# The first layer of an image network on one time scale instead of rounds, with one image kept on chip

## The chip, the cores and the metric

The kernel runs on one core of a Trainium2 chip. It computes two layers of an image network in float32 in one launch. The metric is the device time of one execution in microseconds, as the median of a few runs. Engines are named as in the profile: PE (matrix engine; PEld its weight loads), DVE (vector engine), ACT (scalar engine), POOL, and SP, which issues most DMAs. All engines run their own queue of instructions in order[...].

## What is computed

The input `x` has 4 images of 192 channels and 128 x 128 points. Both layers have the form `x + f(gn(x))`, where `gn` normalises groups of six channels over all points of an image:

```python
x = x + _L0_conv_ref(_gn(x), ...)   # first layer: transforms of the image plane
x = x + _L1_conv_ref(_gn(x), ...)   # second layer: a scan over the 16384 points of an image
return x
```

The first layer is what the change touches:

```python
x1 = c1x1(x, conv1_w)                                   # 192 -> 48 channels
x_0, x_05, x_1 = x1[:, :16], x1[:, 16:32], x1[:, 32:48]
Fre = frft2d(x_05, 0.5)                                 # fractional Fourier transform of the plane
mag, pha = abs(Fre), angle(Fre)
mag_out = c1x1(c3x3(mag * mask1, ...) * mask1 + c1x1(mag * mask2, ...) * mask2, ...)
pha_out = c1x1(pha, ...)
ifrft = abs(frft2d(complex(mag_out * cos(pha_out), mag_out * sin(pha_out)), -0.5))
# x_1: rfft2, a 1x1 convolution of magnitude and of phase, irfft2;  x_0: a 1x1 convolution
return c1x1(concatenate([x_0o, ifrft, x_1o], axis=1), conv2_w)      # 48 -> 192 channels
```

The second layer is a state-space scan (384 inner channels, 16 states) over the points in order, with a normalisation over channels, two projections and a gate around it.

## The kernel before

`layer0` treats an image in four works, each a Python generator that emits some instructions and yields:

- **analysis** (line 266): sixteen pieces of `x` (96 partitions, 2 x 1024 points, 768 KB each) are loaded by SP (`load`, line 196) and their statistics taken on DVE (`bn`, line 202). After all sixteen, `bn_done` (line 215) makes the group statistics, which are folded into the weights of the 1x1 convolution (L284 to L291). Then every piece is convolved (L301) on PE, evacuated by ACT (L305) into one of two `x1` buffers, and stored in the DRAM tensor `d1` from ACT's queue (L311). The last four pieces (`KEEP = 4`) are still on chip from the first pass. The other twelve are loaded again.
- **forward** (line 314): one read of `d1` (`img<-d`, L317), then the transforms on PE (L233, L243) with copies on ACT (L249) and DVE (L251), and `_polar` (L70 to L100: magnitude and phase, much of it on DVE, with a reciprocal at L87). Magnitudes and phases are stored in DRAM (L326, L333).
- **backward** (line 337): the 3x3 and 1x1 convolutions (L263, L373), `_from_polar` (L103 to L119, with five operations of a block on DVE ahead of ACT's sines and two behind), a store and a read with rows and columns exchanged (L397, L425, L417, L453), then the inverse transforms (L432, L440, and L462, L470 for the second kind), and the store `dimg<-img` (L478).
- **synthesis** (line 481): for each of sixteen pieces it reads `d1` and `dimg` into one of two `cat` tiles (L492, L493), projects 48 to 192 channels (L506), adds the result to a piece of `x` loaded once more (L510), takes the statistics that the second layer needs (L205), and stores the sum (`xmid<-xt`, L514, from POOL's queue). At its end `bn_done` makes this image's statistics `st2`.

The pieces of `x` of analysis and synthesis share one pool of seven buffers, `l0x`. The tiles of transforms lie in the pools `l0i`, `l0z`, `l0u`, `l0v` and `l0q`, all opened before any work begins.

The order of emission is set by rounds. `weave` (line 520) takes several works with a number of steps each, spreads the steps evenly, and at the end of the round runs every work to its end. Image 0's analysis comes first and alone. Then round `p` holds backward of image `p - 1`, forward of image `p`, analysis of image `p + 1` and synthesis of image `p - 2`:

```python
for p in range(B + 1):
    works = []
    if p:
        works.append((backward(p - 1, got[p - 1]), 19))
    if p < B:
        works.append((forward(p, got[p]), 9))
    if p + 1 < B:
        works.append((analysis(p + 1, got[p + 1]), 2 * NPIECE + 1))
    if p >= 2:
        works.append((synthesis(p - 2, got[p - 2], []), NPIECE + 1))
    weave(works, early if p == B else None)
```

In the last round the first four pieces of the last synthesis are loaded early, at step 14 of 19 (`LOADS`). A scheduler below takes the order of emission as priority, and from it makes the fixed queue of each engine, which may differ in detail. The last synthesis runs after the rounds, beside the preamble of the second layer (`layer1`: constants, `group_norm`, the first chunk of 512 points). From there on `layer1` follows a plan written out by hand (`PLAN`), under manual scheduling; its loop of scans (`tensor_tensor_scan`, L989) takes the rest of the time.

Of the kernel before, what the change touches and what calls it, by code (L numbers as in the profile page):

```python
# [33 lines left out]
NPIECE = S // ROWS  # L34
# [87 lines left out]
def layer0(tc, x, xmid, st2, w):  # L122

    nc = tc.nc
    B = x.shape[0]
    KEEP = 4
    LOADS = 14
    with ExitStack() as ctx, ExitStack() as inner:
        def pool(name, bufs, ctx=inner, **kw):
            return ctx.enter_context(tc.tile_pool(name=name, bufs=bufs, **kw))  # L130

        kp = pool("l0k", 1, ctx)
        dram = pool("l0d", B, ctx, space=DRAM)
        xp = pool("l0x", 7, ctx)
        sp = pool("l0s", 2, ctx)
        psB = pool("l0r", 2, ctx, space=PSUM)
        cp = pool("l0c", 1)
        fp = pool("l0f", 2)
        imp = pool("l0i", 2)
        zp = pool("l0z", 2)  # L140
        up = pool("l0u", 7)
        vp = pool("l0v", 4)
        qp = pool("l0q", 1)
        psA = pool("l0p", 4, space=PSUM)

        def const(name, cp=cp):
# [46 lines left out]
        def split(v):  # L193
            return v.rearrange("(t p) f -> p t f", p=CH)

        def load(b, p):
            xt = xp.tile([CH, 2, PIECE], F32, name="xt")
            src = x[b].rearrange("c h w -> c (h w)")[:, p * PIECE : (p + 1) * PIECE]
            nc.sync.dma_start(out=xt, in_=split(src))
            return xt  # L200
# [56 lines left out]
        def by_row(d, c0, nch):  # L257
            return d[c0 * S : (c0 + nch) * S, :].rearrange("(c k) l -> k c l", k=S)
# [4 lines left out]
            nc.tensor.matmul(ps[:, 0:n], bd[:, i, :], rhs, start=True, stop=True)  # L263
            return ps[:, 0:n]

        def analysis(b, got):


            st = sp.tile([CH, 2, NPIECE * (PIECE // 512), 6], F32, name="st")
            kept = {}  # L270
            for p in range(NPIECE):
                xt = load(b, p)
                if p >= NPIECE - KEEP:
                    kept[p] = xt
                bn(st, p, xt)
                yield
            gst = sp.tile([CH, 2, 2], F32, name="gst")
            bn_done(st, gst, in_a)

            w1r = fp.tile([CH, 2, 128], F32, name="w1r")
            for t in range(2):
                nc.vector.tensor_scalar(w1r[:, t, :], w1T[:, t, :], gst[:, t, 1:2], None, ALU.mult)  # L284
            ps = psA.tile([128, 512], F32, name="ps")
            for t in range(2):
                nc.tensor.matmul(
                    ps[:, 0:1], w1r[:, t, :], gst[:, t, 0:1], start=t == 0, stop=t == 1
                )
            b1 = fp.tile([128, 1], F32, name="b1")  # L290
            nc.vector.tensor_scalar(b1, ps[:, 0:1], -1.0, None, ALU.mult)  # L291
            d1 = got["d1"] = dram.tile([3 * NC, S * S], F32, name="d1")
            for p in (*range(NPIECE - KEEP, NPIECE), *range(NPIECE - KEEP)):
                xt = kept.pop(p, None) or load(b, p)
                if p % 2 == 0:
                    x1 = fp.tile([128, 2, 512], F32, name="x1")
                ps = psA.tile([128, 512], F32, name="ps")
                for t in range(2):
                    for q in range(2):
                        half = slice(64 * q, 64 * (q + 1))  # L300
                        nc.tensor.matmul(  # L301
                            ps[half], w1r[:, t, half], xt[:, t, q * 512 : (q + 1) * 512],
                            start=t == 0, stop=t == 1,
                        )
                nc.scalar.activation(x1[:, p % 2, :], ps, AF.Identity, bias=b1)  # L305
                if p % 2 == 1:
                    at = d1[:, (p - 1) * PIECE : (p + 1) * PIECE].rearrange(
                        "c (e q f) -> q c e f", e=2, q=2
                    )
                    for q in range(2):  # L310
                        nc.scalar.dma_start(out=at[q], in_=x1[64 * q : 64 * q + 3 * NC])  # L311
                yield

        def forward(b, got):

            xT = imp.tile([128, 2 * NC, S], F32, name="img")
            nc.sync.dma_start(out=xT, in_=got["d1"][NC:, :].rearrange("c (h w) -> h c w", h=S))  # L317

            dm = dmag[b % len(dmag)]
            dp = got["dp"] = dram.tile([NC * S, S], F32, name="dp")  # L320
            for half in range(2):
                mag, pha = yield from spectrum(
                    xT, 0, fr2[:, 0, :], fr2, S, (2 * half, 2 * half + 1)
                )
                for src, dst in ((mag, dm[1 : NC * S + 1, :]), (pha, dp)):
                    nc.sync.dma_start(  # L326
                        out=by_row(dst, 8 * half, 8), in_=src.rearrange("k (c l) -> k c l", c=8)
                    )

            dh = got["dh"] = [dram.tile([NC * S, L], F32, name=f"dh{i}") for i in range(2)]  # L330
            polar = yield from spectrum(xT, NC, rf1, rf2, L, range(4))
            for src, dst in zip(polar, dh):
                nc.sync.dma_start(  # L333
                    out=by_row(dst, 0, NC), in_=src.rearrange("k (c l) -> k c l", c=NC)
                )
# [145 lines left out]
        def synthesis(b, got, early):  # L481

            d1, dimg = got["d1"], got["dimg"].rearrange("c h w -> c (h w)")
            st = sp.tile([CH, 2, NPIECE * (PIECE // 512), 6], F32, name="st2")
            xts = list(early)

            def fetch(p):
                if p < NPIECE:
                    cat = cats[p % 2]
                    for q in range(2):  # L490
                        at = slice(p * PIECE + q * 512, p * PIECE + (q + 1) * 512)
                        nc.sync.dma_start(out=cat[64 * q : 64 * q + NC, :], in_=d1[0:NC, at])  # L492
                        nc.sync.dma_start(out=cat[64 * q + NC : 64 * q + 3 * NC, :], in_=dimg[:, at])  # L493
                if len(early) <= p + len(early) < NPIECE:
                    xts.append(load(b, p + len(early)))

            if early:
                fetch(0)
            for p in range(NPIECE):
                fetch(p + 1 if early else p)  # L500
                xt, cat = xts[p], cats[p % 2]
                for t in range(2):
                    pr = psB.tile([128, 2, 512], F32, name="pr")
                    for q in range(2):
                        rows = slice(64 * q, 64 * q + 3 * NC + 1)
                        nc.tensor.matmul(  # L506
                            pr[0:CH, q, :], w2x[rows, t * CH : (t + 1) * CH], cat[rows, :],
                            start=True, stop=True,
                        )
                    nc.vector.tensor_add(  # L510
                        xt[:, t, :], xt[:, t, :], pr[0:CH].rearrange("p q f -> p (q f)")
                    )
                bn(st, p, xt)
                nc.gpsimd.dma_start(  # L514
                    out=split(xmid[b][:, p * PIECE : (p + 1) * PIECE]), in_=xt
                )
                yield
            bn_done(st, st2[:, b], in_b)

        def weave(works, early=None):  # L520

            n = max(count for _, count in works)
            for i in range(n):
                for work, count in works:
                    for _ in range((i + 1) * count // n - i * count // n):
                        next(work, None)
                if early is not None and i == LOADS:
                    early.extend(load(B - 1, p) for p in range(KEEP))
            for work, _ in works:
                for _ in work:  # L530
                    pass

        got = [{} for _ in range(B)]
        weave([(analysis(0, got[0]), 1)])
        early = []
        for p in range(B + 1):
            works = []
            if p:  # L540
                works.append((backward(p - 1, got[p - 1]), 19))
            if p < B:
                works.append((forward(p, got[p]), 9))
            if p + 1 < B:
                works.append((analysis(p + 1, got[p + 1]), 2 * NPIECE + 1))
            if p >= 2:
                works.append((synthesis(p - 2, got[p - 2], []), NPIECE + 1))
            weave(works, early if p == B else None)
        inner.close()
        yield  # L550
        yield from synthesis(B - 1, got[B - 1], early)
# [730 lines left out]
```

## Time and profile before

| what | value |
|---|---|
| runs of the kernel before | 10828.12, 10829.38, 10840.17 us; median 10829.38 |
| the profiled execution, its own time | 10830.13 us |
| its span, first to last instruction | 10828.4 us |
| mean granted PE clock | 0.957 |
| busy over the span | PE 91%, DVE 94%, ACT 87%, POOL 85% |
| first 1400 us | 293 MB moved by DMA (209 GB/s) of 1417 MB in all |
| in these, most of it | `xt<-in_x` 176 loads of 768 KB; `xmid<-xt` 64 stores of 768 KB |

A row of the table of stages gives the stretch in us, its length, then for each engine the busy time in us with the number of instructions in brackets, and last the granted PE clock (1.00 is full speed), the mean busy share of the 16 DMA engines and the rate in GB/s. A row of a timeline gives start and duration in us, engine, source line, operation, output and inputs with shapes, and the number of instructions merged in it. In square brackets stands how long the engine was idle before it and what ended that. `SPq` is SP's queue issuing DMAs, so its duration is that of issuing, not of the transfer. One matrix product in float32 shows as two MATMUL records, so a piece's convolution (four products) shows as x8.

### The profile page before, as it was taken

Reading aid. Unit: us, or ns where it says so; the run is one execution under the profiler, and the core shown is the slowest. Engines: PE = TensorE matmul, PEld = TensorE weight load, DVE = VectorE, ACT = ScalarE, POOL = GpSimd, SP = SyncE. Lnnn points to the kernel's source line nnn. Section 1 sums busy time; section 2 is a strip of 40 time slices with the busy share of each in tenths; the row PEclk is TensorE's granted clock in tenths of the full one; section 3 lists DMA queues with packets and bytes.
Section 4 is the critical chain, followed back from the end, with each engine's and each line's share of the span. In section 5 each row is a group of like instructions: output and inputs, shape, how many; then the busy total and the mean of one; then the engine's idle time right before and its main releaser. Section 6 shows DMA issues by size and latency. Waiting matters only on the chain.

```text
span 10828.4 us, 170277 instructions
## 1 busy us (share of the span) xinstructions
PE 9879.0 (91%) x55538; PEld 6942.9 (64%) x55538; DVE 10219.2 (94%) x11587; ACT 9404.2 (87%) x19559; POOL 9214.5 (85%) x4214
## 2 busy tenths in 40 slices
PE   4776789999999999999999999999999999999998
PEld 2444366666666666666666666666666666666666
DVE  4666699999999999999999999999999999999999
ACT  1332189999999999999999999999999999999998
POOL 0000089999999999999999999999999999999999
PEclk8888799999999999999999999999999999999999
DMA  8786743443443443443444444444444344344343
GB/s 229 189 227 179 222 137 108 126 127 108 127 124 111 124 125 112 122 126 112 120 127 113 118 127 116 115 127 118 113 127 122 109 127 123 109 127 126 108 127 98
DMA packets 1357320, 1416.75 MB, mean 131 GB/s; under 512 B 920729, under 2 KB 972174, under 8 KB 1355790
## 3 DMA queue, kind: packets, MB, share of 16 engines
q1 hardware_dynamic: 1335950, 1342.94, 44.5%
q0 software_dynamic: 13312, 50.34, 1.4%
q10 hardware_dynamic: 7168, 12.59, 0.4%
q8 instruction: 440, 7.21, 0.3%
q14 instruction: 450, 3.69, 0.1%
HBM read 1230.12 MB, written 155.33 MB: 128 GB/s over the span
## 4 chain that ended last, share of the span: by engine, by line
PE 50%; ACT 19%; DVE 17%; issue 5%; DMA 1%; POOL 0%; SPq 0%; DVEq 0%; POOLq 0%; ACTq 0%
PE ps L799 18%; PE ps L1015 14%; DVE h L989 11%; ACT da L911 6%; PE op L975 5%; DVE op L932 3%; PE ps L1055 3%; ACT dbT L960 3%; ACT L696 2%; ACT op L911 1%; ACT L818 1%; PE ps L1030 1%; ACT zs L818 1%; ACT sT L758 1%; DVE st L732 1%
## 5 line engine op out<-in xcount | busy, mean ns | idle before, releaser
L1002 POOL TENSOR_TENSOR hc<-h,c 128x1024 f32<-128x1024 f32 x3072 | 7202.9, 2367 | 314.5 <-DVE h L989 249.2
L989 DVE TENSOR_TENSOR_SCAN h<-da,carry,op 128x512 f32<-128x512 f32 x4712 | 5821.6, 1265 | 8.6 <-issue 2.9
L911 ACT ACTIVATE da<-dt,c_A_log 128x512 f32<-128x512 f32 x4864 | 3423.7, 751 | 219.5 <-DVE h L989 199.1
L1015 PE MATMUL ps<-ident,hc 128*128 128x128 f32 x24576 | 3221.3, 277 | 4.1 <-POOL hc L1002 4.1
L1015 PEld LDWEIGHTS ps<-ident,hc 128*128 128x128 f32 x24576 | 2866.7, 144 | 411.8 <-issue 402.0
L960 ACT ACTIVATE dbT<-ps,bT 128x128 f32<-128x128 f32 x8192 | 2291.2, 399 | 32.7 <-PE op L975 23.3
L799 PE MATMUL ps<-s,wc 128*128 128x512 f32 x4608 | 2142.3, 596 | 18.8 <-ACT s L784 13.9
L932 DVE TENSOR_TENSOR op<-ps,b 128x512 f32<-128x512 f32 x2816 | 1897.0, 674 | 5.7 <-ACT ps L892 5.7
L975 PE MATMUL op<-ident,dbT 128*128 128x128 f32 x8192 | 1319.6, 292 | 445.3 <-DVE h L989 417.9
L989 DVE TENSOR_TENSOR_SCAN h<-op,carry,db 128x512 f32<-128x512 f32 x1240 | 1547.3, 1267 | 6.9 <-ACT op L911 1.3
L943 POOL TENSOR_TENSOR db<-dtu,b 128x1024 f32<-128x1024 f32 x640 | 1514.1, 2366 | 6.2 <-DMA xmid<-xt 6.2
L975 PEld LDWEIGHTS op<-ident,dbT 128*128 128x128 f32 x8192 | 1034.0, 151 | 745.2 <-DVE h L989 437.3
L799 PEld LDWEIGHTS ps<-s,wc 128*128 128x128 f32 x4608 | 804.0, 190 | 725.0 <-issue 681.2
L911 ACT ACTIVATE op<-dt,c_A_log 128x512 f32<-128x512 f32 x1280 | 928.9, 726 | 14.1 <-DVE h L989 14.1
L1055 PE MATMUL ps<-yg,c_woT 128*96 128x512 f32 x1536 | 700.9, 592 | 0.0
L696 ACT ACT_TABLE_LOAD x511 | 655.6, 1283 | 9.8 <-PEq L1272 0.7
L514 POOL DMA_DIRECT2D xmid<-xt x64 | 41.7, 651 | 576.0 <-DVE xt L510 491.5
L857 POOL TENSOR_TENSOR dtu<-dt,u 128x512 f32<-128x512 f32 x384 | 482.5, 1271 | 0.0
L205 DVE BATCH_NORM_STATS2 st<-xt 96x6 f32<-96x512 f32 x512 | 322.6, 677 | 106.7 <-DMA xt<-in_x 105.5
L78 POOL TENSOR_TENSOR u<-u 128x1024 f32<-128x1024 f32 (+1 forms) x12 | 29.7, 2475 | 453.0 <-ACT u L77 453.0
L1055 PEld LDWEIGHTS ps<-yg,c_woT 128*96 128x96 f32 x1536 | 236.6, 163 | 273.1 <-issue 273.1
L1030 PE MATMUL ps<-ddp,u 128*128 128x128 f32 x3072 | 405.8, 275 | 0.0
(175 smaller groups left out, 10012.2 us busy)
## 6 DMA issues: line engine op xcount, KB each, us to landing
c<-dbc SPq DMA_DIRECT2D x1024, 512.0 KB, 4.9
b<-dbc SPq DMA_DIRECT2D x768, 512.0 KB, 6.1
xt<-in_x SPq DMA_DIRECT2D x176, 768.0 KB, 8.6
xmid<-xt POOLq DMA_DIRECT2D x64, 768.0 KB, 6.2
xm<-xmid SPq DMA_DIRECT2D x128, 384.0 KB, 3.9
carry<-h SPq DMA_DIRECT2D x3072, 1.0 KB, 2.0
xr<-xmid SPq DMA_DIRECT2D x128, 384.0 KB, 3.8
out<-xr SPq DMA_DIRECT2D x128, 384.0 KB, 3.9
```

The lines of the kernel that those rows point to most:

```text
L696: nc.scalar.preload_act_table_set("natural_log_exp_and_others")
L799: nc.tensor.matmul(g["c", j][0], wc[:, j, k, :], rhs, start=k == 0, stop=k == 5)
L911: nc.scalar.activation(da, got[n]["dt", j], AF.Exp, scale=A[:, j, st : st + 1])
L932: nc.vector.tensor_tensor(dbs[s], g["dp", j][0], g["b", k % NG][:, q, :], ALU.mult)
L943: nc.gpsimd.tensor_tensor(db, _bc(g["dtu", j], 1, G), g["b", sg], ALU.mult)
L960: nc.scalar.activation(t[:, blk, :], g["tu", j][0][:, at], AF.Identity, scale=g["bT"][:, blk, st : st + 1],)
L975: nc.tensor.transpose(db[:, blk * 128 : (blk + 1) * 128], t[:, blk, :], ident)
L989: nc.vector.tensor_tensor_scan(h[:, q, :], das.pop(s), dbs.pop(s) if db is None else db[:, q, :], 0.0 if ch == 0 else g["before"][:, j, st ...
L1002: nc.gpsimd.tensor_tensor(hc, h, g["c", sg], ALU.mult)
L1015: nc.tensor.matmul(py[:, blk, :], hc[:, q, blk * 128 : (blk + 1) * 128], ident, start=first, stop=sg == NG - 1 and q == G - 1 and blk == N ...
L1030: nc.tensor.matmul(got[n]["py", j][0][:, blk * 128 : (blk + 1) * 128], got[n]["u", j][:, blk * 128 : (blk + 1) * 128], ddp[:, j, :], start ...
L1055: nc.tensor.matmul(po, woT[:, j, t * CH : (t + 1) * CH], g["yg", j], start=j == 0, stop=False)
```

## The change

Four things change, all in `layer0`:

- Image 0 is kept on chip. For its analysis alone, a second pool `l0y` of nine buffers is opened, so all sixteen pieces have a place (nine there, seven in `l0x`) and no piece is loaded twice. The pools of the transforms are opened only after that, in the same space. The six last pieces are convolved first, then the other ten.
- `weave` and the rounds are gone. Every work has a begin and an end on one time scale, where image `b`'s forward lies from `b + 0.05` to `b + 0.95`, its backward from `b + 1` to `b + 2`, its synthesis from `b + 2` to `b + 2.9`, and its analysis from `b - 1.1` to `b - 0.15` (image 0's runs ahead of all). A work's steps are spread evenly between, and all steps are sorted by time. A round's end no longer runs the works to their ends.
- So analysis begins a tenth of a round sooner and ends 0.15 sooner, forward begins later by 0.05 and ends sooner by as much, and synthesis ends a tenth sooner.
- The early loads of the last synthesis come at 4.74 on that scale.

```diff
-    LOADS = 14
+    ANALYSIS, FORWARD, BACKWARD, SYNTHESIS = (-.1, .85), (.05, .95), (1, 2), (2, 2.9)
+    LAST_LOADS = 0.74
+    XBUFS = 7
...
-        def analysis(b, got):
+        def analysis(b, got, more=None):
...
+            keep = NPIECE if more else KEEP
             for p in range(NPIECE):
-                xt = load(b, p)
-                if p >= NPIECE - KEEP:
+                xt = load(b, p, more if more and p < NPIECE - XBUFS else xp)
+                if p >= NPIECE - keep:
                     kept[p] = xt
...
-            for p in (*range(NPIECE - KEEP, NPIECE), *range(NPIECE - KEEP)):
+            last = NPIECE - (XBUFS // 2 * 2 if more else KEEP)
+            for p in (*range(last, NPIECE), *range(last)):
                 xt = kept.pop(p, None) or load(b, p)
...
+        got = [{} for _ in range(B)]
+        with tc.tile_pool(name="l0y", bufs=NPIECE - XBUFS) as more:
+            for _ in analysis(0, got[0], more):
+                pass
+        imp = pool("l0i", 2)
...
+        works = [(B + LAST_LOADS, B + LAST_LOADS, 1, loads)]
+        for b in range(B):
+            if b:
+                works.append((*(b - 1 + t for t in ANALYSIS), 2 * NPIECE + 1, lambda b=b: analysis(b, got[b])))
+            works.append((*(b + t for t in FORWARD), 9, lambda b=b: forward(b, got[b])))
+            works.append((*(b + t for t in BACKWARD), 19, lambda b=b: backward(b, got[b])))
+            if b < B - 1:
+                works.append((*(b + t for t in SYNTHESIS), NPIECE + 1, lambda b=b: synthesis(b, got[b], [])))
+        steps = sorted(
+            (begin + (i + 1) * (end - begin) / count, n, i)
+            for n, (begin, end, count, _) in enumerate(works) for i in range(count)
+        )
+        running = [make() for *_, make in works]
+        for _, n, i in steps:
+            next(running[n], None)
+            if i + 1 == works[n][2]:
+                for _ in running[n]:
+                    pass
```

More of the change, by code (lines that the diff above doesn't have):

```diff
@@ L133, in layer0 @@
         dram = pool("l0d", B, ctx, space=DRAM)
-        xp = pool("l0x", 7, ctx)
+        xp = pool("l0x", XBUFS, ctx)
         sp = pool("l0s", 2, ctx)
@@ L138, in layer0 @@
         fp = pool("l0f", 2)
[L139 to L143, printed above, removed]
         psA = pool("l0p", 4, space=PSUM)
@@ L194, in split, with load @@
             return v.rearrange("(t p) f -> p t f", p=CH)
-        def load(b, p):
+        def load(b, p, xp=xp):
             xt = xp.tile([CH, 2, PIECE], F32, name="xt")
@@ L518, in synthesis @@
             bn_done(st, st2[:, b], in_b)
[L520 to L530, printed above, removed]
-                    pass
@@ L535, in layer0 @@
[L535 to L548, printed above, removed]
+        got = [{} for _ in range(B)]
@@ new lines, in layer0, with loads @@
+        with tc.tile_pool(name="l0y", bufs=NPIECE - XBUFS) as more:
+            for _ in analysis(0, got[0], more):
+                pass
+        imp = pool("l0i", 2)
+        zp = pool("l0z", 2)
+        up = pool("l0u", 7)
+        vp = pool("l0v", 4)
+        qp = pool("l0q", 1)
+        early = []
+        def loads():
+            early.extend(load(B - 1, p) for p in range(KEEP))
+            yield
+        works = [(B + LAST_LOADS, B + LAST_LOADS, 1, loads)]
[6 more added lines that the diff above has]
+                works.append((*(b + t for t in SYNTHESIS), NPIECE + 1, lambda b=b: synthesis(b, got[b], [])))
```

## The prediction

> **What bounds the kernel now.** I read the forty slices first, then engine busy time by stage, then the timelines of DVE, PE and the SP queue around the stage borders. The stages below are cut where the SP queue issues an image's read (`img<-d`) and its result's store (`dimg<-img`): fill to 129 us, round 0 to 276, round 1 to 526, round 2 to 806, round 3 to 1060, round 4 to 1250, tail to 1397, where the scan loop of the second layer begins.
>
> ```profile
> core 0: us, PE busy (x) PEld busy (x) DVE busy (x) ACT busy (x) POOL busy (x), PEclk, DMA share, GB/s
> 71.00:129.00 58.00, 35.45 (x136) 11.65 (x136) 11.27 (x25) 10.54 (x17) 0.00 (x0) 0.93 0.87 249
> 129.00:276.00 147.00, 86.61 (x345) 49.91 (x346) 83.68 (x111) 43.75 (x61) 7.09 (x3) 0.75 0.86 223
> 276.00:526.00 250.00, 183.87 (x701) 111.55 (x699) 149.18 (x176) 90.74 (x124) 14.14 (x11) 0.84 0.76 183
> 526.00:806.00 280.00, 222.74 (x824) 120.14 (x824) 192.90 (x234) 88.87 (x122) 23.85 (x27) 0.85 0.86 229
> 806.00:1060.00 254.00, 175.40 (x673) 105.20 (x674) 159.78 (x185) 75.25 (x102) 23.32 (x26) 0.84 0.67 180
> 1060.00:1250.00 190.00, 156.10 (x500) 80.26 (x499) 125.77 (x158) 43.64 (x60) 16.48 (x26) 0.83 0.74 204
> 1397.00:10828.00 9431.00, 8925.00 (x52096) 6425.67 (x52096) 9357.77 (x10475) 9018.85 (x19017) 9113.80 (x4096) 0.98 0.42 119
> ```
>
> The last row is 87% of the span, with DVE busy 99% of it. The change doesn't touch it: in the built order of the changed program the second layer's instructions stand as before on every engine. So the whole question is how much earlier than 1397 that loop begins. No engine is full in the first 1397 us; the fill and round 0 have the DMA engines at 0.86 to 0.94 with PE and DVE waiting, rounds 1 to 4 are a mix of chains (PE 62 to 82%, DVE 60 to 69%).
>
> The fill and round 0, on DVE, PE and SP:
>
> ```profile
> 68.02 2.47 DVE L205 BATCH_NORM_STATS2 st<-xt 96x6 f32<-96x512 f32 x4 [1.04 <-DMA xt<-in_x]
> 118.10 2.47 DVE L205 BATCH_NORM_STATS2 st<-xt 96x6 f32<-96x512 f32 x4 [39.77 <-DMA xt<-in_x]
> ...
> 115.12 1.94 PE L301 MATMUL ps<-xt,w1r 96*64 96x512 f32 x8 [2.02 <-DMA xt<-in_x]
> 139.64 3.75 PE L233 MATMUL ps<-c_fr,img 128*128 128x256 f32 x8 [22.58 <-DMA img<-d]
> ...
> 212.40 1.97 PE L301 MATMUL ps<-xt,w1r 96*64 96x512 f32 x2
> ...
> 276.37 0.70 SPq L317 DMA_DIRECT2D img<-d  x1
> ```
>
> Image 0's statistics end at 70.5 us. Its 1x1 convolution (L301) then waits for pieces of x read a second time; DVE stands 39.77 us until image 1's first piece lands at 118. Image 1's convolution starts at 212.40, after its statistics, and the next image can be read at 276.37.
>
> The tail:
>
> ```profile
> 1249.67 0.38 SPq L478 DMA_DIRECT2D dimg<-img  x1
> 1250.16 12.65 SPq L650 DMA_DIRECT2D gd<-dnmr  x2
> 1262.90 0.88 SPq L645 DMA_DIRECT2D dnmr<-nmr  x1
> 1271.72 0.89 SPq L493 DMA_DIRECT2D cat<-dimg  x2
> ```
>
> SP takes 12.65 us over two tiny reads queued behind the dimg store. It is not waiting for synthesis 2: that image's statistics leave DVE at 1258.3, while SP is still held. In round 3 the dimg store, queued behind an image read, took 10.11 us to issue in the same way. So the hold comes from the transfer ahead.
>
> **Part 1, image 0 kept.** Twelve reads of 786 KB disappear (9.44 MB). By the trace, the first loads come one per 3.25 us (statistics at 20.92 to 53.38 us, ten pieces), so 39 us of the loading stream. Of the Trainium skill, "DMA: Bandwidth & Descriptors", section Bandwidth, gives 341 GB/s for 1 MB transfers, which would make it 28 us. The row is this kernel's own pattern (96 partitions, 4 KB pieces), so I take 39.
>
> Where does it show? In the built order, image 1's sixteen loads follow at once. Their buffers come free as image 0's convolution proceeds, first near 81 us (DMA is idle from 77 to 83 today). Between 83 and 117 us twelve reloads arrived beside the d1 stores, 2.85 us each, so sixteen take to about 128, and with the 2.1 MB image read among them to about 137. Image 0's convolution stays paced by its two x1 buffers: ACT waits 3 to 7 us for d1 stores at each second pair today. I take the last landing at 124 instead of 128.9 (bounds 115 and 129), so the image read lands near 135 instead of 139.6.
>
> The changed DVE order puts 59 of image 1's 64 statistics ahead of forward(0)'s first copy. At 137 they are done before that copy is ready (148.46 today, about 144 then), so the wait costs nothing; had the sixteen loads shared one 235 GB/s stream with the d1 stores and the image read (17.8 MB), they would end at 157 and hold forward(0) for some 10 us. Next, image 1's group statistics stand behind the second copy (155.5 today, 151 then) and one polar block up to its reciprocal (1.2 + 1.2 + 0.7 + 1.2 + 6.5 = 10.9 us, after ACT's squares and absolutes, 8 us as today). Convolution starts at 151 + 8 + 10.9 + 2 = 172 instead of 212.4. It then takes the 58 us of today (212.40 to 270.8; its twelve reloads remain). Gain at round 1's start: 40 by this chain, 39 by bytes, 31 in the slow case. I take 38.
>
> The new pools lie in the kept tiles' space; their first user is the image read, which waits for the last convolution anyway, so this costs 0. If not, it is one landing, 2 to 4 us.
>
> **Part 2, one time scale.** No operation is added; order moves. Three places matter.
> - Round 1. Between 336 and 383 us DVE works with some 2 us of idle in all: 17 statistics (0.68 us, 11.5 us), the aggregation (1.9), two from-polar blocks and a polar block. PE waits for it:
>
> ```profile
> 380.18 1.22 PE L432 MATMUL ps<-c_fi_cat,v 128*128 128x256 f32 x2 [9.43 <-DMA v<-df]
> 388.19 2.93 PE L432 MATMUL ps<-c_fi_cat,v 128*128 128x256 f32 x6 [6.78 <-DMA v<-df]
> ```
>
> In the changed order none of image 2's statistics stand there: they come earlier, and eight of its loads are issued before image 1 is read (six today). Saving 11.5 + 1.9 at most, 0 if the loads are late; I take 10.
> - Rounds 2 and 3. The same stretch keeps 18 of 21 statistics in round 2. The borders lose 5 to 10 us of PE waiting, but synthesis statistics now stand on ACT ahead of the last three z copies of the backward transform. If the synthesis is late, those, their matmuls and the dimg store wait behind it; the store is followed by the next synthesis. Worth between -30 and +25 over both rounds; I take 0, as the listed order is otherwise alike.
> - Round 4 and tail. Synthesis 2 ends before backward(3), so its one statistics round trip (1262.90 to 1265.32 us, 2.4 us) leaves SP's queue, and the last inverse units stand without its matmuls between them (1 to 3 us). SP's hold of 11 us behind the store stays, and both `wc` loads now come after it, whose product precedes the last synthesis on DVE (1271 us today). Between -3 and +8; I take 3. Next late is the landing of the store, 12 to 14 us after its issue.
>
> A rule speaks against spreading work: "TensorE: Matmul & The Clock Gate", section HAM oscillation, wants no PE idle gaps over about 3.4 us, as the clock then halves. In this trace, PE ran at a granted 1.00 in the dense 440:520 and 0.61 in 160:200. A convolution moved to a clock of 0.61 would take 32 / 0.61 = 52 us instead of 32 us, 20 more in each of two rounds. In the built order the convolutions still come behind the first inverse unit, in the dense half, so I take 0 and keep the 40 as a bound.
>
> **Sum** against the profiled execution (10830.13 us, span 10828.4, 1.7 outside): 38 + 10 + 0 + 3 = 51, span 10777.4, time 10779.1. The median of the runs is 0.75 below the profiled one: 10778 us, 0.47% faster.
>
> **Rivals.**
> - Rounds compress too (chance 0.18). For it: 5 to 10 us of PE waits at each border and the bubbles above. Another 25 us: 10753.
> - Half is lost again (0.14). Round 2 moves 64 MB at 229 GB/s; its loads and stores set part of its pace, and an earlier start doesn't speed them. With 30 us lost in rounds 2 and 3, the low end above: 10808.
> - Nothing comes (0.06): the reloads are hidden because round 0 is held by forward(0)'s chain. Against it: PE's 22.58 us wait for the image and 32 us wait for image 1's statistics. 10829.
> - Slower (0.08). Synthesis doesn't keep its compressed pace (sixteen pieces took 268 us in round 2, 16.7 us each), and ACT's in-order wait holds the last three inverse units (5.5 us each) plus the 13 us landing behind it: 30 us in each of rounds 2, 3 and 4, 90 in all, against 51: 10829 + 39 = 10868. It turns slower once a round loses 17 us. Against it: synthesis also starts its loads with fewer analysis loads beside them.
>
> **How the numbers follow.** The main case has 0.54, own range 10760 to 10800 (start 31 to 41, round 1 0 to 13, end -3 to 8, the rest of the rounds within 10). A range of 10742 to 10815 leaves out the no-change and slower cases and a little beyond the fast one. Within 0.2% (21.7 us, about what can be told from no change) is 10808 to 10851; the half-lost case straddles its edge. Faster 0.80, same 0.12, slower 0.08.
>
> **What would show it.** Right: image 1's statistics follow image 0's after some 12 us instead of 39.77; its convolution starts near 172, the second image read near 238, the first scan near 1346; no statistics trip between the store and the last synthesis' reads. Wrong: waits of ACT's z copies on the synthesis statistics at the round ends; lower clocks in the convolution; rounds 2 or 3 longer than 280 and 254 us.

## The result, and the profile after

The changed kernel took 10751.42 us as the median of four runs (10745.80 to 10756.00), against 10828.75 us for the kernel before in four runs beside it: a ratio of 0.9929, 95% interval 0.9912 to 0.9946, 77 us faster. Five more runs of it in a later series gave 0.9935 (0.9922 to 0.9947). The forecast was 51 us. The sign and the range were right, but the sum was not right term by term.

The profiled execution took 10754.14 us, span 10752.4 us. First its stages, cut at the same events as before (reads of `img` and stores of `dimg`; columns as in the prediction):

```profile
core 0: us, PE busy (x) PEld busy (x) DVE busy (x) ACT busy (x) POOL busy (x), PEclk, DMA share, GB/s
71.00:129.00 58.00, 38.60 (x136) 12.43 (x136) 32.52 (x60) 10.55 (x17) 0.00 (x0) 0.84 0.80 231
129.00:242.00 113.00, 79.74 (x328) 45.31 (x328) 60.49 (x75) 39.80 (x57) 4.69 (x2) 0.85 0.82 222
242.00:479.00 237.00, 166.10 (x622) 101.02 (x623) 144.11 (x175) 86.02 (x116) 14.76 (x11) 0.82 0.77 194
479.00:745.00 266.00, 218.48 (x826) 119.96 (x825) 188.17 (x225) 89.05 (x122) 24.45 (x27) 0.87 0.86 232
745.00:996.00 251.00, 204.80 (x788) 122.97 (x787) 185.77 (x210) 88.48 (x119) 27.26 (x28) 0.88 0.75 201
996.00:1175.00 179.00, 147.98 (x486) 75.51 (x484) 118.95 (x161) 40.41 (x57) 17.28 (x26) 0.86 0.77 213
```

The second layer is as it was: from the last `dimg` store to the end of the span, 9578.7 us before and 9577.8 after. So the gain is all ahead of that store, in the first layer. The same events in both traces say where:

| event, us | before | after | sooner by |
|---|---|---|---|
| read of image 0's `img` | 128.9 | 129.2 | -0.3 |
| first convolution of image 1 | 212.4 | 174.7 | 37.8 |
| read of image 1's `img` | 276.4 | 242.5 | 33.9 |
| store of `dimg` 0 | 518.3 | 501.7 | 16.6 |
| read of image 2's `img` | 526.4 | 478.6 | 47.8 |
| store of `dimg` 1 | 806.4 | 765.9 | 40.5 |
| store of `dimg` 2 | 1059.6 | 995.6 | 64.0 |
| store of `dimg` 3 | 1249.7 | 1174.6 | 75.0 |
| first scan of the second layer | 1395.1 | 1316.0 | 79.1 |

At the start 34 us are won, 17 of them are lost again by the first `dimg` store, and then 47 come in rounds 2 and 3, and 15 behind them. In a second profile of the changed kernel (c1 below) the reads, the stores and the scan lie up to 5.2 us from those of this table, so a few us of one row say nothing. (With the new order an image's read no longer stands beside the `dimg` store of the image before, so "rounds" from here on means the stretches between `dimg` stores.)

The start, DVE and PE of the trace after (start, duration, engine, line, operation, idle before it):

```profile
86.32 2.47 DVE L202 BATCH_NORM_STATS2 st<-xt 96x6 f32<-96x512 f32 x4 [8.95 <-DMA xt<-in_x]
144.39 2.47 DVE L202 BATCH_NORM_STATS2 st<-xt 96x6 f32<-96x512 f32 x4 [13.89 <-DMA xt<-in_x]
...
140.17 3.75 PE L230 MATMUL ps<-c_fr,img 128*128 128x256 f32 x8 [24.60 <-DMA img<-d]
174.65 1.97 PE L300 MATMUL ps<-xt,w1r 96*64 96x512 f32 x2
```

DVE's idle of 39.77 us is down to 8.95. But a new wait of 13.89 us stands at 144: three of image 1's sixteen loads are queued on SP behind the read of `img` at 129.2, and arrive with it. PE still waits 24.60 us for that read, as it did 22.58 before.

The tail, the first scan of the kernel before, then SP's queue and the first scan of the changed kernel:

```profile
1395.10 2.33 DVE L989 TENSOR_TENSOR_SCAN h<-da,op 128x512 f32<-128x512 f32 x2 [4.83 <-ACT da L911]
...
1174.63 0.49 SPq L477 DMA_DIRECT2D dimg<-img  x1
1175.21 9.47 SPq L653 DMA_DIRECT2D gd<-dnmr  x3
...
1315.99 2.33 DVE L992 TENSOR_TENSOR_SCAN h<-da,op 128x512 f32<-128x512 f32 x2 [5.39 <-ACT da L914]
```

From the store to the first scan it was 145.4 us and is 141.4. The statistics no longer interrupt SP, and its hold behind the store is 9.47 us instead of 12.65. These 4 us do not reach the end: from the first scan to the end it is 9433.3 us before and 9436.4 after (9436.6 in the second profile of the changed kernel).

Rounds 2 and 3 together, from `dimg` 0 to `dimg` 2. What PE waited for there (total us, number of waits, longest), before and then after:

```profile
PE ps L432 <- DMA v<-df: 49.6, 4, 18.4
PE ps L263 <- DMA v<-dh: 25.8, 3, 14.0
PE ps L263 <- DVE f L388: 11.5, 5, 5.5
```

```profile
PE pr L505 <- DVE xt L509: 21.3, 8, 9.9
PE ps L431 <- DMA v<-df: 16.3, 3, 7.5
PE ps L260 <- DMA v<-dh: 11.8, 4, 5.3
```

`v<-df` and `v<-dh` are the two places where backward reads again from DRAM what was stored there, rows and columns exchanged. PE waited 75.4 us for them in two rounds, and 28.1 us now. Of these 47.3 us, 21.8 came back as waits of synthesis on DVE (`xt`, 2.6 us before and 24.4 after), so 25.5 are left. Another 10.3 are waits on group statistics (`mv` and `gs_d`, 12.9 before and 2.6 after), and the rest is spread over smaller rows. Summed over all rows, PE's waits fell from 137.5 to 89.4 us. In the same stretches PE was busy 404.40 us (of 542) and 404.54 us (of 494). The length of a stretch is PE's busy time and its waits together, so this says where the 48 us went, and not yet why.

A row names only the last link of a wait. Round 3 of the trace before, with SP, DVE and PE in order of time:

```profile
887.41 1.58 SPq L397 DMA_DIRECT2D df<-v  x2
...
915.52 1.23 DVE L112 SCALAR_TENSOR_TENSOR v<-v 128x1040 f32<-128x1040 f32 x1
916.78 0.39 SPq L425 DMA_DIRECT2D v<-df  x1
922.63 1.19 PE L432 MATMUL ps<-c_fi_cat,v 128*128 128x256 f32 x2 [18.37 <-DMA v<-df]
...
929.65 2.09 SPq L417 DMA_DIRECT2D di<-v  x2
931.83 3.26 SPq L425 DMA_DIRECT2D v<-df  x3
936.35 2.93 PE L432 MATMUL ps<-c_fi_cat,v 128*128 128x256 f32 x6 [12.53 <-DMA v<-df]
```

The last `df` stores were issued by 889 us, but the first read of them is issued only at 916.78, when DVE has just ended an operation of `_from_polar` on the tiles of `dh` (915.52 + 1.23 = 916.75). The other three reads stand behind the two `di` stores, which store the result of that same block. From the issue of a read to PE's start it is 5.9 and 4.5 us, of waits of 18.37 and 12.53 us. The changed kernel has the same pattern: in its round 3 the last `df` store is issued at 842.59, DVE's operation ends at 867.25, and the first read is issued at 867.28. The transfer itself did not become shorter: from issue to landing the reads of `df` took 5.4 us before and 5.2 us after, in the median. So what PE waits for under the name of `df` is in large part DVE's work on `dh`. By the code these tiles all come from the four buffers of `l0v`, which the `dh` pair and its two temporaries fill, so a read of `df` has no place sooner. No run with more such buffers was made. From the second read of `dh` to the `di` stores it took 36.5 and 40.6 us in rounds 2 and 3 before, and 35.1 and 31.4 us after.

### The profile page after: what moved, and what is told of

Its sections match the earlier page's. It is cut to its first block, busy times and chain, and to the rows that moved or that the text cites. A ratio compares the mean times of both kernels' runs of the same rounds, so it can differ in the third digit from the quotient of the medians.

```text
span 10752.4 us, 170232 instructions
## 1 busy us (share of the span) xinstructions
PE 9881.9 (92%) x55538; PEld 6950.1 (65%) x55538; DVE 10220.8 (95%) x11587; ACT 9413.5 (88%) x19560; POOL 9222.7 (86%) x4214
## 4 chain that ended last, share of the span: by engine, by line
PE 51%; ACT 18%; DVE 18%; issue 5%; DMA 1%; POOL 0%; SPq 0%; DVEq 0%; POOLq 0%; ACTq 0%
PE ps L802 19%; PE ps L1018 14%; DVE h L992 11%; ACT da L914 6%; PE op L978 6%; DVE op L935 3%; PE ps L1058 3%; ACT dbT L963 3%; ACT L699 2%; PE ps L1033 2%; ACT op L914 1%; ACT L821 1%; ACT zs L821 1%; DVE st L735 1%; ACT sT L761 1%
## 5 line engine op out<-in xcount | busy, mean ns | idle before, releaser
L808 PE MATMUL ps<-s,wz 128*128 128x512 f32 x768 | 393.8, 594 | 0.0
```

## The experiments

Each kernel was timed four to seven times beside the kernel before, in three series, each on another chip: e1, e2, e3 and e7, then c1 and e4 to e6, then e8 to e11. This table has the gain (difference of the medians of one series, and the ratio with its interval), and from the profile of each the read of image 1's `img`, the length of rounds 2 and 3 (`dimg` 0 to `dimg` 2), PE's waits in it, those for `df` and `dh` among them, and the store of `dimg` 3.

| kernel | faster by, us | ratio (95%) | `img` 1 at | rounds 2+3 | PE waits | `df`+`dh` | `dimg` 3 at |
|---|---|---|---|---|---|---|---|
| before | - | - | 276.4 | 541.3 | 137.5 | 75.4 | 1249.7 |
| e1 image 0 kept, rounds | 28 | 0.9973 (0.9963-0.9984) | 235.5 | 537.2 | 136.7 | 75.5 | 1197.7 |
| e2 time scale, image 0 not kept | 47 | 0.9959 (0.9946-0.9971) | 270.8 | 492.8 | 88.4 | 27.2 | 1190.2 |
| e3 both, no shifts | 51 | 0.9955 (0.9942-0.9967) | 241.6 | 525.3 | 121.0 | 74.3 | 1187.9 |
| e4 only analysis shifted | 57 | 0.9949 (0.9936-0.9961) | 238.1 | 505.6 | 113.5 | 68.2 | 1183.7 |
| e5 only forward shifted | 34 | 0.9970 (0.9959-0.9982) | 239.2 | 540.3 | 125.3 | 68.7 | 1207.6 |
| e6 only synthesis shortened | 49 | 0.9952 (0.9939-0.9966) | 240.3 | 533.3 | 118.9 | 48.3 | 1193.7 |
| c1 the changed kernel again | 70 | 0.9935 (0.9922-0.9947) | 242.0 | 495.6 | 88.4 | 28.9 | 1169.5 |
| e7 four `x1` buffers | 81 | 0.9926 (0.9913-0.9940) | 226.3 | 488.9 | 87.4 | 27.8 | 1147.6 |
| e8 e3 + early loads | 62 | 0.9944 (0.9931-0.9958) | 245.2 | 524.5 | 121.1 | 69.6 | 1201.4 |
| e9 changed + early loads | 69 | 0.9937 (0.9925-0.9950) | 237.4 | 506.9 | 108.6 | 33.0 | 1189.0 |
| e10 e7 + early loads | 87 | 0.9924 (0.9912-0.9936) | 234.2 | 504.4 | 106.2 | 32.4 | 1177.8 |
| e11 e7 + analysis earlier | 116 | 0.9895 (0.9882-0.9909) | 235.4 | 470.8 | 73.7 | 18.3 | 1146.7 |

The theory after the first comparison: about half of the gain is the start (image 0 kept), the other half comes from the time scale in rounds 2 to 4. Rival: all of it comes from the start, and the rest follows.

### The two parts, each alone (e1, e2)

e1 keeps image 0, but weaves in rounds as before: the new head and the old loop. e2 is the changed kernel with one argument less:

```diff
-            for _ in analysis(0, got[0], more):
+            for _ in analysis(0, got[0]):
```

> Image 0 of x kept on the chip, but the works still woven in rounds as in the kernel before. If the start gives about half of the 77 us and the time scale the rest, this is 34 to 40 us faster than before (about 10791). If all of it comes from the start, it is 70 to 80 us faster (about 10752). If the kept image only lets a bound appear that the time scale then removes, it is under 15 us faster. By the prediction's own sum: 38 us faster.

> The time scale with its shifts, but image 0 handled as before (4 pieces kept, 12 loaded again). If the two parts add up, this is 35 to 43 us faster than before (about 10790). By the prediction's own sum (10 + 0 + 3): 13 us faster (about 10816). If the time scale needs the kept image, it is within 5 us of before.

Measured: 28 us (17 to 40 by the interval) and 47 us. They sum to 75, and the change has 77 and 70. The parts add up, within these intervals. "All from the start" is refuted, since the time scale does as much without it. For e2 the prediction's own 13 us is refuted: its interval holds 31 to 58 us. (It lies above all three of its expectations, nearest to that of parts that add up.) Rounds 2 and 3 tell why, since PE's waits in e1 are those of before, line by line:

```profile
PE ps L430 <- DMA v<-df: 49.5, 4, 18.8
PE ps L259 <- DMA v<-dh: 26.0, 3, 13.9
```

and those of e2 are those of the changed kernel:

```profile
PE ps L431 <- DMA v<-df: 16.2, 3, 7.6
PE ps L260 <- DMA v<-dh: 11.0, 4, 5.3
```

e1 is under the 34 to 40 us expected, while its profile shows `img` 1 read 41 us sooner and `dimg` 3 stored 52 us sooner. The two profiled executions compared there lie at opposite ends of their scatter: e1's took 10776.66 us (median 10790.78), that of before 10830.13 us (median in e1's series 10819.21). For sizes I therefore use the medians, and the traces for the place.

### The time scale without shifts, and one shift at a time (e3 to e6)

```diff
-    ANALYSIS, FORWARD, BACKWARD, SYNTHESIS = (-.1, .85), (.05, .95), (1, 2), (2, 2.9)
+    ANALYSIS, FORWARD, BACKWARD, SYNTHESIS = (0, 1), (0, 1), (1, 2), (2, 3)            # e3
+    ANALYSIS, FORWARD, BACKWARD, SYNTHESIS = (-.1, .85), (0, 1), (1, 2), (2, 3)        # e4
+    ANALYSIS, FORWARD, BACKWARD, SYNTHESIS = (0, 1), (.05, .95), (1, 2), (2, 3)        # e5
+    ANALYSIS, FORWARD, BACKWARD, SYNTHESIS = (0, 1), (0, 1), (1, 2), (2, 2.9)          # e6
```

> Image 0 kept and one time scale, but each work over the whole unit that was its round: analysis and forward over 0 to 1, synthesis over 2 to 3. If only the rounds' ends (each round emptied before the next begins) cost the time, this is within 8 us of the changed kernel (about 10755). If the shifts of analysis, forward and synthesis against each other bring it, this is as slow as the kept image in rounds, 10785 to 10795.

> Image 0 kept and one time scale, of the three shifts only that of analysis (-0.1 to 0.85). If the sooner statistics and convolution of the next image bring what the shifts bring (some 26 us between 49 without shifts and 77 with all), this is 70 to 80 us faster than before. If the shifts matter only together, or synthesis brings it, it is 45 to 55 us faster.

> Image 0 kept and one time scale, only forward shifted (0.05 to 0.95). If the start of forward inside the unit is what matters (its first steps no longer beside the border, its last done before backward begins), 60 to 75 us faster than before. If the analysis brings it, 40 to 55 us.

> Image 0 kept and one time scale, only synthesis shortened (2 to 2.9). By the prediction's reasons this brings nothing before the last units: 49 to 54 us faster than before. If the synthesis's last steps delay the border's work in units 2 and 3, 60 to 75 us faster.

> The changed kernel once more, beside the three runs that follow. 72 to 80 us faster than before (10740 to 10748 where before takes 10820); its profile shows how far one execution's stages lie from another's: within 5 us at the reads of img if the start is what varies, within 2 us from the last dimg store to the end.

e3 gave 51 us, between its two expectations. Against e1 it has the same start and the same waits for `df` and `dh` (74.3 us); what it loses of PE's waits is 16 us in rounds 2 and 3, and of these 11 are those on group statistics. The rows of these before (e1 has the same), and then the one of e3:

```profile
PE pr L63 <- DVE gs_d L61: 5.8, 1, 5.8
PE pr L56 <- DVE mv L218: 4.4, 1, 4.4
PE ps L63 <- DVE gs_d L61: 2.7, 1, 2.7
```

```profile
PE ps L63 <- DVE gs_d L61: 2.3, 1, 2.3
```

So dropping the rounds brings some 20 us: 51 against 28, in one series. The remaining 20 to 26 us are the shifts'. c1 met its expectation but for the median (70, not 72 to 80).

None of the shifts does it alone. Against the 51 us of e3, analysis alone has 57 and synthesis alone 49, both within the intervals. Forward alone has 34, less than either of its expectations, and all its runs are slower than all of e3 (10782.78 to 10792.22 us against 10761.35 to 10776.88, with the kernel before at the same time in both series): it costs 17 us. All three together cut PE's waits by another 32 us. The expectation that the sooner analysis is the whole of it fell.

The profiles show what a single shift does. In e4 rounds 2 and 3 are 20 us shorter than in e3, but round 1 (from the read of image 1's `img` to the first `dimg` store) is 18 us longer, 259.8 us against 242.1. Work moved from the later rounds into it: in rounds 2 and 3 DVE is busy 350 us instead of 368, and PE 391.51 us instead of 403.94, at a granted clock of 0.88 instead of 0.86. With synthesis shortened alone (e6) `df` and `dh` fall to 48 us, but `xt` rises by 18, PE's busy time rises from 404 to 414 us, and the rounds become 8 us longer. In e5 they are 15 us longer, 11 of it in PE's busy time. So one row does not decide, nor do the waits alone. Which pair of shifts is enough was not tried.

### Where the start is held (e7)

`analysis` takes the pool of `x1` as an argument (`out`, else `fp` as before):

```diff
-        with tc.tile_pool(name="l0y", bufs=NPIECE - XBUFS) as more:
-            for _ in analysis(0, got[0], more):
+        with (
+            tc.tile_pool(name="l0y", bufs=NPIECE - XBUFS) as more,
+            tc.tile_pool(name="l0o", bufs=4) as out,
+        ):
+            for _ in analysis(0, got[0], more, out):
```

> The changed kernel with four instead of two buffers for image 0's x1 (the tile between the convolution's evictions and the two d1 stores), in a pool given back with the kept pieces. If the stores' round trips pace image 0's convolution (ScalarE waits of 2.6, 6.8, 2.0, 6.2, 1.0 and 7.7 us on them), the image's read is issued at 115 to 124 instead of 129 us and the whole is 4 to 13 us faster than the changed kernel. If the bytes of stores and loads together pace it, the read stays at 128 to 130 us and the time is within 3 us of the changed kernel.

In the changed kernel ACT's evictions of image 0's convolution wait for the stores of `d1` to give a buffer back; two of them:

```profile
109.48 1.27 ACT L304 ACTIVATE x<-ps,b 128x512 f32<-128x512 f32 x2 [6.24 <-DMA d<-x]
...
120.64 1.27 ACT L304 ACTIVATE x<-ps,b 128x512 f32<-128x512 f32 x2 [7.68 <-DMA d<-x]
```

With four buffers the last eviction starts at 105.74, and no wait but PE's own pace is left:

```profile
105.74 0.69 ACT L304 ACTIVATE x<-ps,b 128x512 f32<-128x512 f32 x1 [1.03 <-PE ps L300]
```

The read of image 0's `img` is issued at 115.4, 121.0 and 120.7 us in the three kernels with four buffers, and at 124.1 to 129.2 (mean 126.9) in the nine with two and image 0 kept: 8 us sooner in the mean. The stores' round trip paced the convolution, not the bytes. In time it is 81 us against 77 and 70, which the intervals do not tell apart. But e10 has 87 us against 69 for e9, with all runs of one below all of the other in one series: 18 us.

### The reads again, ahead of their use (e8, e9, e10)

In `backward` the two loads of `dh`, and then the four of `df`, are issued first, with an empty step after each, so that other works stand between load and use (21 steps instead of 19):

```diff
             for src in dh:
                 t = vp.tile([128, NC * L], F32, name="v")
                 nc.sync.dma_start(out=t, in_=src.rearrange("(p r) l -> p (r l)", r=16))
+                inner.append(t)
+            yield
+            for t in inner:
...
+            fqs = []
             for half in range(2):
...
                     nc.sync.dma_start(out=t, in_=by_row(src, 8 * half, 8))
+                fqs.append(fq)
+            yield
+            for half, fq in enumerate(fqs):
                 for q in range(4):
```

> The kernel of e3 (image 0 kept, one time scale, no shifts) with one thing more: backward issues both loads of dh, and then all four loads of df, ahead of their use and gives one empty step to the other works before each use. TensorE waited 110 us for these two in e3's works and 59 us in the changed kernel's. If the shifts help by putting other works' matmuls into these two round trips, the waits fall below 70 us and this is 65 to 90 us faster than before (10730 to 10755), as fast as the changed kernel without its shifts. If the wait only moves to another step, it stays within 8 us of e3, 43 to 57 us faster than before.

> The changed kernel with the same early loads and two empty steps in backward. If the 59 us of waits for df and dh that are left in it are still on the path, they fall to 20 to 35 us and this is 10 to 30 us faster than the changed kernel (80 to 100 us faster than before). If synthesis's waits (xt, 42 us) have become the bound, it is within 6 us of the changed kernel, 65 to 80 us faster than before.

> Four buffers for image 0's x1 (e7) and the early loads (e9) together. If both gains stand and add, 8 to 14 us faster than e9. If the early loads bring nothing, as fast as e7 was: 78 to 84 us faster than before.

e8 does not decide the question it was made for: over the stretch that its expectation counts, the waits for `dh` and `df` are 105.9 us, against 110.5 in e3, and rounds 2 and 3 stayed at 525 us. Its trace says why the edit did so little. In round 2 the first read of `df` is issued at 618.42, still behind DVE's operation on `dh` that ends at 617.86, and the other three at 625.86, still behind the `di` stores at 623.69. The reads stand earlier in the code, but nothing let them start earlier. Its 62 us lie between the two expectations, and its median of 10772 us is close to that of e3 (10768); only the kernel before took 15 us more in its series. e9 shows a moved wait plainly. In rounds 2 and 3 of its trace:

```profile
PE ps L437 <- DMA v<-df: 21.2, 2, 13.2
...
PE ps L56 <- DVE mv L215: 9.5, 1, 9.5
...
PE ps L260 <- DMA v<-dp: 7.6, 2, 4.8
```

Synthesis's wait for `xt` fell from 24 to 8 us, but waits on statistics (`mv`) and on `dp` appeared, and the sum rose from 89 to 109 us. It is 69 us faster than before, as the changed kernel is, which was the second of its expectations. e10 is 18 us faster than e9, more than the 8 to 14 expected, and level with e7 (87 against 81, the intervals overlap). Early loads as these edits made them bring nothing here.

### Analysis earlier still (e11)

```diff
-    ANALYSIS, FORWARD, BACKWARD, SYNTHESIS = (-.1, .85), (.05, .95), (1, 2), (2, 2.9)
+    ANALYSIS, FORWARD, BACKWARD, SYNTHESIS = (-.2, .75), (.05, .95), (1, 2), (2, 2.9)  # and e7's x1 buffers
```

> The kernel of e7 (four x1 buffers) with the analysis shifted further ahead, -0.2 to 0.75. If an earlier analysis goes on paying as from e3 to e4, 84 to 95 us faster than before. If it now pushes backward of the image before behind it (the first dimg store came 16 to 18 us later with the shift), 65 to 80 us faster.

The best of all: 10718.82 us against 10834.76, 116 us faster than before, more than either expectation, with all four of its runs below the fastest of e7 (10724.27 against 10725.80). How much of it is the shift is less sure. By the gains it is 35 us on e7, by the medians alone 19.5, since the kernel before took 15 us more in this series. PE's waits in rounds 2 and 3 are 73.7 us, `df` and `dh` 18.3 of them, and the two rounds take 470.8 us:

```profile
PE ps L260 <- DMA v<-dh: 9.4, 3, 4.9
PE ps L431 <- DMA v<-df: 8.9, 3, 7.5
```

The fear that it pushes backward behind it is real too. At the read of image 1's `img` stands a single wait of PE that no other kernel has, and the first `dimg` store comes 15 us later than in e7 (497.6 against 482.7).

```profile
257.46 2.04 PE L260 MATMUL ps<-magQ,c_bd 128*128 128x512 f32 x2 [40.19 <-DVE magQ L354]
```

Rounds 2 and 3, 18 us shorter than in e7, make up for that: at the last `dimg` store the two profiles are 1 us apart. The profile of e7 is that of its fastest run and this one that of the slowest of e11, so where the gain in the medians lies these two do not show.

## Why the prediction was right in sign and wrong in its terms

Against the terms 38, 10, 0 and 3 the trace has 34, -17, 47 and 15. The range was met in part by luck, since the two largest errors, -27 and +47, have opposite signs.

**The start: 38, by the trace 34, alone 28 in time.** The mechanism was right. DVE's idle fell to 8.95 us (some 12 expected), image 1's convolution started at 174.65 (172), the read of its `img` came at 242.47 (238). Two steps on the way were wrong and nearly without cost. "I take the last landing at 124" was not met: the pacing by two `x1` buffers that the same passage names held the read at 129.2, the upper bound, and e7 shows what it hid. And image 1's statistics ended at 154, not 137, since I let all its loads share one stream where three are queued behind the `img` read; forward's first copy came at 149.84 against 148.46, so the wait was covered, as expected. Of the order of 10 us of the 38 are not found in the time of e1 (28, with 17 to 40), which the scatter of single executions leaves open.

**Round 1: "I take 10" was minus 17.** This step failed in its argument. The seventeen statistics did leave the stretch. But what DVE did there was not only those, and something else came in:

```profile
339.01 6.54 DVE L87 RECIPROCAL u<-u 128x1024 f32<-128x1024 f32 x1
...
356.99 1.22 PE L431 MATMUL ps<-c_fi_cat,v 128*128 128x256 f32 x2 [9.53 <-DMA v<-df]
367.05 2.93 PE L431 MATMUL ps<-c_fi_cat,v 128*128 128x256 f32 x6 [8.84 <-DMA v<-df]
```

A polar block of forward with its 6.54 us reciprocal now stands there, and PE's two waits are 9.53 and 8.84 us, where they were 9.43 and 6.78. Round 1 takes 259.3 us instead of 241.9 until the `dimg` store, since more of image 2's work lies in it: DVE is busy 161.5 us instead of 141.5, and PE's waits rose from 64.3 to 79.2 us. It is the shift of analysis that does this: e4, with that shift alone, has 259.8 us here, and e3, without shifts, 242.1. The next `img` read is 47.8 us sooner for it. I judged the round by one engine's work in one stretch, and left out what the emptied place is filled with.

**Rounds 2 and 3: "I take 0" was plus 47.** This is the step that failed most, in size, and beyond its bound of 25. The reason given was that "the listed order is otherwise alike". Counted by instructions it was (416 on DVE in these rounds instead of 419), but PE's waits are not the same in another order. The profile before showed 49.6 us of them for `df` and 25.8 for `dh` in two rounds. I had two of them on the page in round 1 and took them for a matter of DVE, which the times of the reads bear out; but I did not ask what the same wait costs in rounds 2 and 3 (18.37 and 12.53 us in round 3) and put its change at nothing. A part of the 47 is paid for in round 1: over rounds 1 to 3 together 10 us were forecast and 30 measured. The feared loss, ACT's z copies behind the synthesis statistics, did not come: PE's waits on `zi` went from 13.5 to 10.4 us. Nor did the cold clock of the rule that I had set against the change: over rounds 2 and 3 the granted clock went from 0.85 to 0.87 and PE's busy time stayed at 404 us, so the 40 us kept as a bound were not called on. The rival "rounds compress too" (10753) described what happened, with 10 us from the waits on statistics and more from a place it did not name, the waits for `df` and `dh`.

**Round 4 and tail: 3, measured 15.** The tail alone is 4, by the parts named: the statistics trip left SP's queue, the hold of about 10 us stayed. But these 4 do not reach the end of the execution. The other 11 us are round 4 (190.1 to 179.0, and 173.9 in the second profile), where PE no longer has this wait of the kernel before:

```profile
PE pr L56 <- DVE mv L218: 7.4, 1, 7.4
```

That gain I had put at 1 to 3. One reading was off without effect: PE's busy share in rounds 1 to 4, given as 62 to 82%, is 69 to 82% by the table shown beside it.

**What is shown and what is not.** Shown: the two parts add up within their intervals (e1, e2); rounds 2 and 3 became shorter in PE's waits, with its busy time unchanged (the profile); dropping the rounds removes the waits on group statistics, and the shifts together most of those on `df` and `dh`, of which nearly half come back as waits for `xt` (e1, e3 and the changed kernel); the transfers of `df` are no shorter, and their reads start when DVE's work on `dh` lets them (the traces). Not shown: which change of the order shortened the waits, and whether more buffers for these tiles would do the same. e8 was to test what covers the reads, and its edit could not move those of `df`. Why forward shifted alone costs 17 us is open too.

## What to carry to other kernels

When works are interleaved on in-order queues, sum for each stage what an engine on the path waits for, row by row, and then follow the largest row back behind its last link: here PE waited for a read, the read for DVE, while the store of its data had been issued 28 us before. An order that seems alike in counts can differ in just these waits. Do not credit a stretch that is emptied before asking what moves in. Look for two-buffer tiles whose release is a DMA store, since there two more buffers brought the next read 8 us sooner for no work; and try the constants of an interleaving on the chip: together with these buffers, the best of those tried here (e11) is another 33 to 46 us faster than the change.

## What the runs showed of the hardware that was not expected

- The same instructions do not give the same start. In nine profiled executions with the same code up to there, image 0's `img` read was issued between 124.1 and 129.2 us. The second layer took 9575.0 to 9579.0 us in all fourteen profiles (from the last `dimg` store to the end of the span).
- PE's busy time in rounds 2 and 3 lay between 391.51 us (e4, granted clock 0.88) and 414.80 us (e5, 0.85), and did not follow its waits: the kernel before had 404.40 us at 0.85 with 137.5 us of waits, the changed kernel 404.54 us at 0.87 with 89.4. How much of that is the clock and how much other work in the stretch was not separated.
- A `dimg` store issued right behind an `img` read took 10.11 us to issue (before, round 3) and 9.57 us (e1), and 0.38 to 0.50 us in the other 54 cases of the fourteen profiles. In the tail, where two or three tiny reads stand behind the `dimg` store, SP's hold lay between 7.31 us (e4) and 12.65 us (before). What makes it so different was not tried.
